# Graph attention on one core: which heads' probabilities VectorE turns, tile by tile, and exponentials that write a second buffer

## The chip, the core and the metric

The kernel runs on one core of a Trainium2 chip. Its time is the device time of one execution in microseconds (us), the median of several runs. The engines named below are TensorE (PE in the profile, with PEld for its weight loads), VectorE (DVE), ScalarE (ACT), GpSimd (POOL) and SyncE (SP), which here only issues DMAs.

## The reference

There are 16 graphs of 1024 nodes with 256 features, and two layers. Layer 0 is attention with 8 heads of 32, masked by the adjacency matrix; layer 1 weighs edges by a product of normed nodes. Both end in a softmax over 1024 columns and a weighted sum.

```
h = relu(layernorm(x))
Q, K, V = proj(Wq, bq), proj(Wk, bk), proj(Wv, bv)          # 8 heads of 32
scores = where(adj == 0, -inf, Q K^T * 32**-0.5)
x = x + (softmax(scores) V) Wo^T + bo
h = relu(layernorm(x))
e_k = leaky_relu((h * a_k) h^T);  scores = e_(adj-1), or -9e15 where adj == 0
x = x + softmax(scores) h
```

The change is in layer 0, between softmax and the product with V.

## The kernel before

**Tiles and steps.** Each graph is cut into 8 tiles of 128 rows (t = 0 to 7). The main loop runs over all 128 tiles, and inside it over 8 steps, one for each head h. The order of the work is written out by hand in this loop: every engine gets its instructions in the order in which the loop records them, and waits are put in where a buffer or a value needs it. Several tiles are in work at once: `now` makes scores, `was` is the tile before it, whose output is finished in steps 0 to 5, `edge` and `edge_was` are layer 1 of tiles nine and ten places back, and `piece` prepares layer 0's keys and values nine places ahead.

**One head.** In step h, TensorE makes the scores of head h (line 455), and VectorE adds the mask, takes the maximum and writes p (`softmax_max`, line 467). In step h + 1, ScalarE makes the exponential of p in place and its sum (`softmax_exp`, line 475). In step h + 2, p is turned, since the product with V needs the columns on the partitions. There are two ways to turn it:

- by TensorE: 8 transposes of 128 x 128 (line 574) into PSUM, which ScalarE copies out in two halves (line 575);
- by VectorE: one transposition of 32 x 32 blocks (`turn_blocks`, line 376) into one of three `blocks` buffers, after which SyncE issues four DMAs of 128 KB (`place_blocks`, line 381) that bring the blocks to their places in pT.

The second way leaves the columns in another order than the first. V is therefore stored in two orders: heads 0, 1, 4 and 5 in the one that suits VectorE's way, heads 2, 3, 6 and 7 in the plain one. `BY_BLOCKS = (0, 1, 4, 5)` says which heads go by VectorE, in every tile.

**Two gathers.** `combine(g)` (line 510) multiplies the turned heads of group g with V: 128 small matmuls for heads 0 to 3 in step 7 of the tile, for heads 4 to 7 in step 3 of the next one. In step 3 the order on ScalarE is the exponential of head 2, `recT` (line 504, the turned reciprocals of `was`), the bend of layer 1 (line 648), a copy to `mirror` (line 630), the flag of the next adjacency tile (line 447), and in step 4 the exponential of head 3. combine(1) writes the PSUM bank that `recT` is copied from. After it, VectorE makes oT (line 520) and TensorE the product with Wo (line 525); VectorE adds the rest (line 531) and takes statistics for the norm.

**Keys.** Each graph has 8 key tiles of 512 KB, one buffer for each head. They are loaded by SyncE (line 355) at the seam between two graphs: for heads 0 to 3 in tile 7 of the graph before, in steps 3, 4, 5 and 6, for heads 4 to 7 in tile 0, in steps 0, 2, 3 and 4. The queries of the next tile are loaded in step 3 (line 422). All these loads stand in one queue with the placing DMAs, the stores of the results (line 691) and of layer 0's output (line 536).

**Buffers.** p has 4 buffers, used in turn; pT has 7.

Of the kernel before, what the change touches and what calls it, by code (L numbers as in the profile page):

```python
# [8 lines left out]
F32 = mybir.dt.float32  # L9
# [4 lines left out]
AF = mybir.ActivationFunctionType  # L14
# [3 lines left out]
P = 128  # L18
HEADS = 8
HD = 32  # L20
# [3 lines left out]
SLOPE = 0.2  # L24
NEG_INF = -9000000000000000.0
MASKED = -1e30
BY_BLOCKS = (0, 1, 4, 5)


def place_of(h):  # L30
# [12 lines left out]
def gnn_kernel(  # L43
# [18 lines left out]
    nc = tc.nc  # L62
    B, N, D = x.shape
# [4 lines left out]
    NB = P // HD  # L68
# [10 lines left out]
    work = ctx.enter_context(tc.tile_pool(name="work", bufs=2))  # L79
# [330 lines left out]
    class Attend:  # L410
# [61 lines left out]

        def softmax_exp(self, h):
            p, nmx = self.probs[h]
            nc.scalar.activation(p, p, AF.Exp, bias=nmx, scale=-1.0, accum_out=self.sums[:, h : h + 1])  # L475

        def turn(self, h, half):
            if half == 0:
# [291 lines left out]
    with tc.manual_schedule():  # L770
# [48 lines left out]
        for s in range(B * NT + 1):  # L819
            b, t = divmod(s, NT)  # L820
# [8 lines left out]
            for h in range(HEADS):  # L829
                ending, eh = (now, h - 1) if h >= 1 else (was, HEADS - 1)  # L830
                turning, th = (now, h - 2) if h >= 2 else (was, HEADS + h - 2)
# [36 lines left out]
                if h == 3:  # L868
# [3 lines left out]
                        piece_was.biased()  # L872
                    if was:
                        was.combined()
                if turning and th in BY_BLOCKS:
                    turning.turn_blocks(th)
                    turning.place_blocks(th)
                elif turning:
                    turning.turn(th, 0)
                    turning.turn(th, 1)  # L880
# [75 lines left out]
            gone, was, now, nxt = was, now, nxt, nxt2  # L956
# [86 lines left out]
```

## Time and profile before

| | us |
|---|---|
| median of 3 runs | 3142.49 |
| lowest, highest | 3139.09, 3142.89 |
| the profiled execution | 3143.69 |
| its span | 3141.9 |
| busy in it: TensorE | 2941.3 (94%) |
| ScalarE | 2598.8 (83%) |
| VectorE | 2512.8 (80%) |
| GpSimd | 2172.4 (69%) |

The length of a tile, from the starts of line 467 for head 0, is on average over graphs 1 to 14: 29.1 us for tile 0, then 23.6, 23.1, 22.8, 22.6, 22.6, 22.4, and 22.3 for tile 7. In graph 0, where layer 1 has no work yet, tiles last 19.9 to 21.7 us.

Some durations of one instruction, mean: maximum of a head 1207 ns, exponential 1155 ns, VectorE's turn 1238 ns, TensorE's transpose 273 ns (eight of them overlap to 1.04 us), a copy of half a head 590 ns.

How to read the profile: busy shares are averages over tiles that have different limits, so the tiles at the seam and those in the middle have to be looked at by themselves. A row of the time line has the start in us, the duration in us, the engine and line, the operation, what it writes and reads, how many instructions are merged in it, and in brackets how long the engine was idle before it and what ended that. "SPq" is SyncE's queue; its duration is that of the issue, not of the transfer.

### The profile page before, as it was taken

How to read it: one execution, taken by the hardware profiler on the slowest of the kernel's cores; microseconds unless marked ns; L12 is line 12 of the kernel's file. 1: busy time of each engine (PE TensorE's matmuls, PEld its weight loads, DVE VectorE, ACT ScalarE, POOL GpSimd, SP SyncE). 2: the span in 40 equal slices, each digit the busy share in tenths (PEclk: the TensorE clock that was granted, in tenths of full speed). 3: DMA queues.
4: the chain of work that ended last, by engine and by line, in shares of the span. 5: the costliest groups of instructions: out<-in, count | busy, mean ns of one | idle time of the engine just before them, and what ended most of it. 6: DMA issues, size and time to landing. Idle time of an engine off the chain costs nothing. (4 is left out here: it accounts for less than half of the span.)

```text
span 3141.9 us, 95789 instructions
## 1 busy us (share of the span) xinstructions
PE 2941.3 (94%) x36210; PEld 2202.9 (70%) x36210; DVE 2512.8 (80%) x4391; ACT 2598.8 (83%) x5157; POOL 2172.4 (69%) x2995
## 2 busy tenths in 40 slices
PE   5888999899999999999999999999999999998987
PEld 3666777677676777777777676777767777676663
DVE  4777888788787887878888787888878788787874
ACT  3888989889888988889889898888978888787871
POOL 2666777777777776777777777777767777675542
PEclk8999999999999999999999999999999999999999
DMA  6676787877878787787877878787787877777663
GB/s 214 208 245 212 230 272 220 270 217 230 255 229 263 223 263 225 226 268 223 270 227 235 251 234 257 228 258 229 234 261 215 271 223 227 245 232 239 185 174 96
DMA packets 634692, 729.22 MB, mean 232 GB/s; under 512 B 67376, under 2 KB 565424, under 8 KB 634224
## 3 DMA queue, kind: packets, MB, share of 16 engines
q1 hardware_dynamic: 565152, 510.86, 54.5%
q0 software_dynamic: 66960, 210.04, 20.5%
q8 instruction: 291, 4.77, 0.6%
q10 hardware_dynamic: 2112, 2.10, 0.2%
q14 instruction: 177, 1.45, 0.1%
HBM read 252.98 MB, written 134.22 MB: 123 GB/s over the span
## 5 line engine op out<-in xcount | busy, mean ns | idle before, releaser
L467 DVE CUSTOM_DVE_ANT_0 p<-s,neg 128x1024 f32<-128x1024 f32 x1024 | 1235.6, 1207 | 274.5 <-PE s L455 241.3
L475 ACT ACTIVATE p<-p,nmx 128x1024 f32<-128x1024 f32 x1024 | 1182.2, 1155 | 205.0 <-DVE nmx L467 202.5
L455 PE MATMUL s<-k,qt 128*128 128x512 f32 x2048 | 764.9, 455 | 107.9 <-DMA k<-kd 72.5
L376 DVE STREAM_TRANSPOSE blocks<-p 128x1024 f32<-128x1024 f32 x520 | 643.7, 1238 | 20.5 <-ACT p L663 10.6
L575 ACT COPY pT<-trp 128x512 f32<-128x512 f32 x1024 | 547.0, 590 | 106.2 <-PE trp L574 106.2
L510 PE MATMUL acc<-pT,v 128*32 128x128 f32 x16384 | 559.0, 281 | 37.1 <-DMA pT<-blocks 22.1
L510 PEld LDWEIGHTS acc<-pT,v 128*32 128x32 f32 x16384 | 472.6, 113 | 156.5 <-issue 82.9
L574 PE MATMUL trp<-ident,p 128*128 128x128 f32 x4096 | 531.2, 273 | 1.6 <-ACT pT L575 1.5
L574 PEld LDWEIGHTS trp<-ident,p 128*128 128x128 f32 x4096 | 478.1, 140 | 73.2 <-ACT pT L575 3.1
L435 POOL TENSOR_SCALAR neg<-adj 128x1024 bf16<-128x1024 int32 x128 | 467.6, 3653 | 79.5 <-ACT neg L447 70.2
L681 PE MATMUL acc<-h,pT 128*32 128x256 f32 x8192 | 494.7, 383 | 8.8 <-DVE ot L690 8.8
L455 PEld LDWEIGHTS s<-k,qt 128*128 128x128 f32 x2048 | 324.3, 192 | 215.5 <-issue 79.5
L681 PEld LDWEIGHTS acc<-h,pT 128*32 128x32 f32 x8192 | 241.8, 110 | 211.9 <-issue 63.8
L659 POOL TENSOR_TENSOR sel<-sel,less 128x1024 f32<-128x1024 f32 x120 | 286.6, 2388 | 64.9 <-ACT less L648 44.9
L616 PE MATMUL s<-h1T,ha 128*128 128x512 f32 (+2 forms) x744 | 272.8, 490 | 2.6 <-ACT h1T L553 1.3
L657 POOL TENSOR_SCALAR less<-top 128x1 f32<-128x1 f32 x120 | 31.6, 264 | 274.5 <-DVE top L639 274.5
L319 POOL DMA_DIRECT2D qd<-halves x240 | 177.0, 777 | 58.7 <-POOL halves L309 31.8
L494 POOL COPY wide<-rec 128x256 f32<-128x256 f32 x128 | 53.9, 421 | 226.5 <-DVE rec L492 226.5
L475 ACT ACTIVATION_READ_ACCUMULATOR p<-p,nmx 128x1 f32 x1024 | 202.7, 198 | 0.0
L325 POOL DMA_DIRECT2D kd<-halves x240 | 171.7, 764 | 35.4 <-POOL halves L309 35.4
L309 POOL TENSOR_TENSOR halves<-full,halves 128x256 fp32r<-128x256 f32 x240 | 176.3, 735 | 20.6
L648 ACT ACTIVATE less<-sel 128x1024 f32<-128x1024 f32 x120 | 127.0, 1058 | 65.6 <-DVE top L639 65.6
(120 smaller groups left out, 4238.8 us busy)
## 6 DMA issues: line engine op xcount, KB each, us to landing
pT<-blocks SPq DMA_DIRECT2D x2560, 128.0 KB, 3.6
k<-kd SPq DMA_DIRECT2D x128, 512.0 KB, 6.1
qt<-qd SPq DMA_DIRECT2D x128, 512.0 KB, 4.4
adj<-in_adj POOLq DMA_DIRECT2D x127, 512.0 KB, 5.1
qd<-halves POOLq DMA_DIRECT2D x240, 256.0 KB, 3.0
kd<-halves POOLq DMA_DIRECT2D x240, 128.0 KB, 4.0
xb<-in_x POOLq DMA_DIRECT2D x128, 128.0 KB, 4.4
x1d<-x SPq DMA_DIRECT2D x128, 128.0 KB, 4.0
```

What stands on the lines that cost most here:

```text
L319: nc.gpsimd.dma_start(out=qds[self.b][self.first, oc].rearrange("p u w n -> p u (w n)"), in_=halves.unsqueeze(1).to_broadcast([P, 2, 2 * P]),)
L376: nc.vector.transpose(blocks.rearrange("p b j q -> p j b q"), p)
L435: nc.gpsimd.tensor_scalar(self.neg, self.adj, 0.0, MASKED, ALU.is_equal, ALU.mult)
L455: nc.tensor.matmul(self.ps[:, cols], lhsT=self.qt[:, h, :], rhs=keysets[self.b][h][:, cols], start=True, stop=True,)
L467: nc.vector.tensor_tensor_reduce(out=p, in0=sides[h in (4, 6)], in1=self.neg, scale=-SCALE, scalar=FLOOR, op0=ALU.add, op1=ALU.min, accum_ ...
L475: nc.scalar.activation(p, p, AF.Exp, bias=nmx, scale=-1.0, accum_out=self.sums[:, h : h + 1])
L510: nc.tensor.matmul(sums_place[r * HD : (r + 1) * HD, g * P : (g + 1) * P], lhsT=vs[self.b][:, j, place_of(h) : place_of(h) + HD], rhs=self ...
L574: nc.tensor.transpose(tr[:, j, :], p[:, jj * P : (jj + 1) * P], ident)
L575: copy(pT[:, half * 4 : half * 4 + 4, :], tr)
L616: nc.tensor.matmul(self.side[:, cols], lhsT=self.ha[:, c, :], rhs=h1T[:, c, cols], start=(c == 0), stop=(c == NC - 1),)
L659: nc.gpsimd.tensor_tensor(self.sel, self.sel, self.less, ALU.subtract)
L681: nc.tensor.matmul(sums_place[a * HD : (a + 1) * HD, :], lhsT=self.pT[:, j, a], rhs=h1s[self.b][:, j, :], start=(j == 0), stop=(j == NT - 1),)
```

## The change

The heads that VectorE turns now depend on the tile: heads 0 and 1 in tile 7, heads 4 and 5 in tile 0, heads 0, 1, 2, 4 and 5 in tiles 1 to 6. V's two orders stay as they are (`MIXED`). A head that is turned in the way that V's order is not made for has its columns put into the right order by the exponential: it reads p and writes a second buffer of the same four in the other order, instead of working in place. That concerns head 2 in tiles 1 to 6, heads 4 and 5 in tile 7, heads 0 and 1 in tile 0: ten exponentials of each graph's 64.

```diff
-BY_BLOCKS = (0, 1, 4, 5)
+MIXED = (0, 1, 4, 5)
+BY_BLOCKS = {7: (0, 1), 0: (4, 5), 1: (0, 1, 2, 4, 5), 2: (0, 1, 2, 4, 5), 3: (0, 1, 2, 4, 5), 4: (0, 1, 2, 4, 5), 5: (0, 1, 2, 4, 5), 6: (0, 1, 2, 4, 5)}
+
+
+def by_blocks(t):
+    return BY_BLOCKS.get(t, MIXED)
...
         def softmax_exp(self, h):
             p, nmx = self.probs[h]
-            nc.scalar.activation(p, p, AF.Exp, bias=nmx, scale=-1.0, accum_out=self.sums[:, h : h + 1])
+            to, of = p, p
+            if (h in MIXED) != (h in by_blocks(self.t)):
+                was = p
+                p = work.tile([P, N], F32, tag="p", bufs=4)
+                orders = "p (j q b) -> p j b q", "p (j b q) -> p j b q"
+                if h not in MIXED:
+                    orders = "p (j b q) -> p j q b", "p (j q b) -> p j q b"
+                to, of = (a.rearrange(order, b=NB, q=HD) for a, order in zip((p, was), orders))
+                self.probs[h] = p, nmx
+            nc.scalar.activation(to, of, AF.Exp, bias=nmx, scale=-1.0, accum_out=self.sums[:, h : h + 1])
...
-                if turning and th in BY_BLOCKS:
+                if turning and th in by_blocks(turning.t):
                     turning.turn_blocks(th)
                     turning.place_blocks(th)
                 elif turning:
```

In these orders b counts 4 and q counts 32: head 2 writes with 32 elements between neighbours, the four others with 4.

## The prediction

> **What bounds the kernel now.** I read four views in this order: the busy time by stretches of one graph's end, the time line of one tile, the SyncE queue, and the waits. Tile t (0 to 7) and head h (0 to 7) are the loops' numbers; "combine(1)" and "combine(0)" are the two gathers of line 510.
>
> The first view has one row for each of four neighbouring tiles (6, 7, then 0 and 1 of the next graph): stretch, its length, busy time of TensorE, weight loads, VectorE, ScalarE, GpSimd, then granted clock, DMA share, GB/s.
>
> ```profile
> 1122.20:1144.30 22.10, 21.99 (x285) 16.81 (x284) 19.37 (x34) 19.94 (x40) 15.65 (x20) 1.00 0.72 219
> 1144.30:1166.90 22.60, 21.93 (x286) 16.99 (x285) 19.54 (x34) 19.92 (x41) 18.86 (x29) 1.00 0.92 286
> 1167.00:1197.40 30.40, 24.81 (x286) 19.31 (x285) 19.56 (x34) 20.08 (x39) 20.65 (x30) 0.89 0.93 320
> 1197.40:1221.40 24.00, 23.86 (x286) 17.27 (x285) 19.70 (x35) 21.00 (x43) 15.08 (x21) 1.00 0.59 169
> ```
>
> Two regimes stand there. In tiles 1 to 7 TensorE is busy nearly throughout (21.99 of 22.10 us). In tile 0 it stands still for 5.6 us, at a clock of 0.89 and a DMA share of 0.93, although its work is the same. What it waits for there:
>
> ```profile
> PE s L455 <- DMA k<-kd: 72.5, 36, 5.8
> PE acc L510 <- DMA pT<-blocks: 22.1, 25, 2.2
> ```
>
> The next graph's keys come late because their loads stand in SyncE's queue behind the placing of heads turned by VectorE (four DMAs of about 0.62 us issue each):
>
> ```profile
> 1164.59 2.85 SPq L381 DMA_DIRECT2D pT<-blocks  x4
> 1167.48 0.63 SPq L536 DMA_DIRECT2D x1d<-x  x1
> 1168.16 0.52 SPq L355 DMA_DIRECT2D k<-kd  x1
> 1168.79 3.67 SPq L381 DMA_DIRECT2D pT<-blocks  x4
> 1172.56 0.93 SPq L355 DMA_DIRECT2D k<-kd  x1
> ```
>
> These fours are heads 4 and 5 of tile 7. The key behind the first lands at 1175.6, and scores(3) waits 2.35 us for it.
>
> In a middle tile the bound is not TensorE alone. Step 3 of a tile 6:
>
> ```profile
> 1127.93 1.24 DVE L376 STREAM_TRANSPOSE blocks<-p 128x1024 f32<-128x1024 f32 x1
> ...
> 1128.11 1.15 ACT L475 ACTIVATE p<-p,nmx 128x1024 f32<-128x1024 f32 x1 [0.41 <-DVE nmx L467]
> ...
> 1129.29 0.37 ACT L504 COPY recT<-acc 128x256 f32<-128x256 f32 x1
> 1129.71 1.78 PEld L510 LDWEIGHTS acc<-pT,v 128*32 128x32 f32 x61 [0.43 <-ACT recT L504]
> ```
>
> The first row is head 0's turn. The exponential of head 2 starts while it runs; recT follows on ScalarE, and combine(1) starts 0.05 us after recT. So this exponential is two instructions ahead of TensorE's next work.
>
> **The change, part by part.** I sum against the profiled execution (3143.7 us, span 3141.9), which is 1.2 us above the median shown, 3142.5.
>
> *Middle tiles (1 to 6 of 16 graphs: 96).* Head 2 goes from TensorE to VectorE.
>
> The added wait. In the changed program the exponential of head 2 writes a new p, and with four p in turn this is the place of head 0 of the same tile: the built program makes it wait for head 0's turn, the first row above. That ends 1.06 us after the exponential starts today; with 0.1 us for the signal (the gap from a maximum's end to its exponential) it starts 1.16 us later. Queued behind it on ScalarE are recT, the bend, the mirror copy, the flag and exp(3); combine(1) waits for recT, the scores of head 4 for the mirror copy. Today recT itself starts some time after exp(2) ends, because it waits for line 500: from the start times of lines 475 and 504, 0.76 us in tile 1, 0.35 in tiles 2 to 5, 0.03 in tile 6, where 0.03 is no slack. So combine(1) moves by 0.43, 0.84 and 1.16 us: mean (0.43 + 4 x 0.84 + 1.16) / 6 = **+0.83 us**.
>
> What is saved behind it, counted from combine(1)'s start. Eight transposes (1.04 us, 0.87 from their start to the next one's) leave TensorE, and two copies of 0.59 leave ScalarE. But the output product of line 525, next on TensorE, needs oT: oT starts at +2.30 and takes 0.42, so with 0.14 for the signal the product starts at +2.86 instead of +3.53. TensorE gains 0.67 and would reach combine(0) at +11.28 instead of +11.95 (median of the middle tiles). The rest of the 0.87 is a wait for oT that the transposes covered.
>
> What is late next: head 2 must now land by DMA before combine(0).
>
> ```profile
> 1133.73 2.49 SPq L381 DMA_DIRECT2D pT<-blocks  x4
> 1136.32 0.54 SPq L422 DMA_DIRECT2D qt<-qd  x1
> ```
>
> Head 1's four and the next queries fill SyncE from +4.02 to +7.15 (combine(1) is at 1129.71). VectorE turns head 2 after the maximum of head 4, from about +5.0 to +6.2, so it is ready before SyncE; its four DMAs issue from +7.2 to +9.7, the last at +9.1. Landing after issue:
>
> ```profile
> DMA to landing us min/median/max: 2.4/3.6/8.8
> ```
>
> That gives +11.5 to +12.7; heads 4 and 5, in a fuller queue, land 3.4 us after their last issue ends, which would be +13.1. I take +12.25: the queries just ahead land 4.2 us after their issue, at +10.8, DMAs land in their order, and the four follow at some 0.35 us each. So combine(0) comes at +12.25 instead of +11.95, **+0.30 us** (ends: -0.67, TensorE alone, and +1.15). VectorE's added 1.24 us (19.4 busy of 22.1) goes first into the 0.78 us it is idle before line 531 and delays the maximum of head 5 to +7.75 from +7.33; the scores of head 7, which need its place, stand at +10.6, so this costs nothing.
>
> Sum: 0.83 + 0.30 = 1.13 us, times 96 = **+108 us** (ends: 0.16 and 1.98 us, +15 and +190).
>
> The new orders of writing. 160 exponentials write in steps: head 2 with 128 bytes between elements, heads 0, 1, 4, 5 with 16. The nearest row is the mirror copy, which writes in 16-byte steps, beside a plain copy (mean ns after the busy time):
>
> ```profile
> L575 ACT COPY pT<-trp 128x512 f32<-128x512 f32 x1024 | 547.0, 590 | 106.2 <-PE trp L574 106.2
> L630 ACT COPY mirror<-s 128x512 f32<-128x512 f32 x64 | 36.4, 569 | 2.6 <-PE s L616 2.6
> ```
>
> No penalty at 16 bytes, so I take nothing. No row writes in 128-byte steps: the upper end is an estimate, the exponential's 1155 ns twice, +1.16 us each; the lower end is -0.09, the difference to the Relu of line 648, which does not write in place (1058). [...]
>
> *Tiles 7 and 0.* Heads 4, 5 of tile 7 and 0, 1 of tile 0 go to TensorE: eight transposes each, 1.04 us, with two copies on ScalarE (1.07 together). TensorE is the bound there, so each costs 1.04 (ends 0.87 and 1.2, where the copies set the pace): 64 heads x 1.04 = +67. Their exponentials find their place free long before. Sixteen placing DMAs leave the queue between these keys: the key issued at 1168.2 can go at about 1164.6, right behind the stores, and the next one after it instead of at 1172.6, before the scores need them; 2.1 MB less compete. Tile 0 lasts 29.4 us on average in graphs 1 to 15 (starts of line 467), 7.1 above tile 7's 22.3; I let 6.5 of it go (ends 5 and 7.1; part of it is the 0.89 clock): 15 x 6.5 = -98. Together **-31 us** (ends -51 and +2).
>
> Sum: 3143.7 + 108 - 31 = 3220.7, so **3220 us**, 2.5% slower.
>
> **Rivals.** (1) The boundary pays, which ends on the other side: head 2 lands in the shortest time seen, so TensorE alone counts in the middle tiles: 96 x 0.16 = +15, and the boundary gives about -38: 3121 us. It decides from 0.40 us per middle tile (38/96), that is a last landing before +11.5. For it: 2.4 us has been seen. Against it: that is the minimum, with queries just ahead. (2) Head 2 lands as late as heads 4 and 5: combine(0) at +13.1: 96 x 0.85 = 82 more, 3302 us. For it: the queries ahead; against it: head 1 lands 2.2 us after its last issue. (3) Stepped writing is dear: 96 x 1.16 = 111 more, 3332 us. Against it: the mirror row. (4) Both sides cancel: about 3145 us, with 0.4 us per middle tile. That the change does not do what it says is excluded: the built program has 32 more turns on VectorE and the waits named above.
>
> **How the numbers follow.** Forecast 0.62, rival 1 0.12, rival 2 0.12, rival 3 0.08, rival 4 0.06. A measurement of this kernel tells 0.2% (6 us) from no change. Slower: 0.62 + 0.12 + 0.08 = 0.82; same 0.06; faster 0.12. The range 3140 to 3310 holds the forecast with most of its own ends and rivals 2 and 4; outside are rivals 1 and 3, 2 in 10.
>
> **What would show it.** Right: in tiles 1 to 6 the third exponential starts after VectorE's turn, idle some 1.5 us before it; combine(1) waits longer for recT; combine(0) waits for pT from blocks; these tiles last near 23.7 us; tile 0 falls to about 25, tile 7 rises to about 24.4; the wait for keys nearly vanishes. Wrong: middle tiles of 22.6 us or less; the stepped exponentials far from 1.15 us; tile 0 still near 29.

## The result, and the profile after

| | us |
|---|---|
| before, median of 4 runs | 3142.69 (3139.09 to 3148.50) |
| after, median of 4 runs | 3616.28 (3608.71 to 3641.63) |
| ratio | 1.1525, 95% interval 1.1472 to 1.1578 |
| the profiled execution after | 3618.44, span 3616.6 |

The change makes the kernel 15% slower. The sign was forecast, the size was not: 3220 us, with 3140 to 3310 as the range.

In the changed program the lines of the code stand lower: the maximum is line 472, the exponential 489, VectorE's turn 381, the placing 386, the queries' load 427, the combines 524, recT 518, oT 534, the mirror copy 644.

Where the time went can be added up from the starts of line 472 for head 0. Over all 16 graphs, tiles 1 to 6 are longer by 495.6 us, tile 7 by 20.3, tile 0 is shorter by 42.5, and the stretch before the first tile is longer by 1.3; together 474.7, the difference of the two profiled spans (tile 7 includes what follows the last one). On average over graphs 1 to 14 the tiles last (us):

| tile | 0 | 1 | 2 | 3 | 4 | 5 | 6 | 7 |
|---|---|---|---|---|---|---|---|---|
| before | 29.1 | 23.6 | 23.1 | 22.8 | 22.6 | 22.6 | 22.4 | 22.3 |
| after | 26.6 | 28.9 | 28.2 | 26.5 | 26.2 | 27.2 | 27.9 | 23.8 |

A middle tile lasts 27.48 us instead of 22.85, so **4.63 us more** where the prediction had 1.13. The busy time by stretches answers to the first view of the prediction; these are tiles 5, 6 and 7 of one graph and 0 and 1 of the next (length, TensorE, weight loads, VectorE, ScalarE, GpSimd, clock, DMA share, GB/s):

```profile
1286.00:1314.10 28.10, 23.17 (x276) 16.78 (x274) 20.31 (x35) 20.12 (x38) 18.89 (x26) 0.95 0.78 237
1314.10:1339.10 25.00, 22.09 (x278) 16.65 (x277) 20.33 (x36) 20.08 (x38) 14.05 (x19) 0.98 0.62 176
1339.10:1363.30 24.20, 23.66 (x303) 18.78 (x302) 17.41 (x33) 22.73 (x43) 18.45 (x27) 1.00 0.92 290
1363.30:1389.70 26.40, 23.42 (x303) 17.97 (x301) 17.31 (x32) 24.02 (x45) 18.06 (x26) 1.00 0.64 217
1389.70:1418.10 28.40, 24.99 (x276) 17.69 (x275) 20.52 (x35) 20.86 (x41) 19.19 (x27) 0.94 0.75 221
```

The two regimes have changed places. Tile 0 (fourth row) stands still for 3.0 us at a clock of 1.00, where it was 5.6 at 0.89. The middle tiles, which were full, stand still instead: in the first row TensorE works 23.17 us of 28.10, in the last 24.99 of 28.40. The waits say for what (total, times, longest):

```profile
PE acc L524 <- DMA pT<-blocks: 301.7, 113, 7.2
...
PEld acc L524 <- ACT recT L518: 247.5, 128, 3.2
...
ACT p L489 <- DVE blocks L381: 135.8, 96, 2.0
```

The wait for keys, 72.5 us before, is no longer in that list. In its place the gathers wait 301.7 us for placing, head 2's above all (22.1 before, for the placing of others), and recT costs them four times as much as before (62.2). The last row is the new wait of the prediction, in all 96 middle tiles.

The time line of the first of these tiles, step 3 on ScalarE, VectorE and TensorE:

```profile
1291.69 1.24 DVE L381 STREAM_TRANSPOSE blocks<-p 128x1024 f32<-128x1024 f32 x1
...
1292.97 2.10 ACT L489 ACTIVATE p<-p,nmx 128x1024 f32<-128x1024 f32 x1 [1.51 <-DVE blocks L381]
...
1294.93 0.36 ACT L518 COPY recT<-acc 128x256 f32<-128x256 f32 x1
...
1295.34 2.16 PE L524 MATMUL acc<-pT,v 128*32 128x128 f32 x64 [1.54 <-ACT recT L518]
```

ScalarE waits for head 0's turn, as forecast; but then the exponential takes 2.10 us, not 1.15. Next, SyncE's queue in the same tile, with the queries' load and the placing of head 2 behind it:

```profile
1301.89 0.54 SPq L427 DMA_DIRECT2D qt<-qd  x1
1302.60 2.56 SPq L386 DMA_DIRECT2D pT<-blocks  x4
```

The first gather of a middle tile before the change, and then TensorE's rows for it in this tile:

```profile
1141.67 1.95 PE L510 MATMUL acc<-pT,v 128*32 128x128 f32 x64
```

```profile
1306.64 0.41 PE L524 MATMUL acc<-pT,v 128*32 128x128 f32 x4
1310.32 2.50 PE L524 MATMUL acc<-pT,v 128*32 128x128 f32 x60 [3.27 <-DMA pT<-blocks]
```

combine(0) is ready at 1306.64, 11.30 us after combine(1) began (the forecast said 11.28; the median of the middle tiles is 11.30). It does four of its 64 matmuls and then stands for 3.27 us: the four DMAs, issued from 1302.60 to 1305.16, land between 1307.80 and 1310.19. What the DMA engines and the clock did meanwhile, in the same columns as above:

```profile
1297.50:1301.50 4.00, 4.00 (x37) 2.87 (x40) 3.86 (x6) 3.54 (x9) 3.92 (x3) 1.00 0.29 75
1301.50:1304.00 2.50, 2.50 (x40) 1.29 (x36) 2.40 (x6) 1.72 (x6) 2.35 (x3) 1.00 0.70 194
1304.00:1307.00 3.00, 3.00 (x38) 1.74 (x29) 2.80 (x7) 2.84 (x5) 2.70 (x6) 1.00 0.97 310
1307.00:1310.30 3.30, 0.05 (x2) 0.01 (x1) 2.46 (x4) 2.42 (x6) 2.96 (x8) 1.00 1.01 277
1310.30:1313.00 2.70, 2.68 (x61) 2.32 (x62) 0.00 (x0) 0.00 (x0) 2.19 (x4) 0.73 1.00 363
```

From 1304 on the DMA share is 0.97 to 1.01. After the standstill the granted clock averages 0.73 over 2.7 us; it falls to 0.50 at 1311.55 and is back at 1.00 at 1314.97. On average over the middle tiles of graphs 1 to 14 the longest gap in combine(0), from one matmul's start to the next, is 2.83 us, and from first to last matmul it lasts 5.61 us instead of 1.95. The tile shown is one of the worse: head 2's last DMA lands 14.85 us after combine(1) began, 14.12 on average.

The clock is a part of the loss by itself. In 52 of the 96 middle tiles it falls to 0.50, in none before, and it stays there for 293 us of them in all. Between the first tile and the last it falls 58 times, 35 times for 3.41 us, 19 for 6.83, once for 10.24 and three times for 13.65. By the profile's busy times, TensorE was busy for 0.49 or less of the 3.41 us ahead of each fall; of the 861 other stretches of that length, after which the clock stayed at 1.00, TensorE was busy for at least half in 838. In the tile shown TensorE was busy for 1.23 of the 3.41 us ahead of the fall at 1311.55, so a standstill of 3.27 us, shorter than such a stretch, was enough there.

### The profile page after: what moved, and what is told of

Same layout as the page of the kernel before. It is cut to its first block, busy times and chain, and to the rows that moved or that the text cites. A ratio compares the mean times of both kernels' runs of the same rounds, so it can differ in the third digit from the quotient of the medians.

```text
span 3616.6 us, 95204 instructions
## 1 busy us (share of the span) xinstructions
PE 3041.2 (84%) x35954; PEld 2252.7 (62%) x35954; DVE 2534.2 (70%) x4423; ACT 2696.7 (75%) x5093; POOL 2169.4 (60%) x2995
## 5 line engine op out<-in xcount | busy, mean ns | idle before, releaser
L489 ACT ACTIVATE p<-p,nmx 128x1024 f32<-128x1024 f32 x1024 | 1347.3, 1316 | 272.9 <-DVE nmx L472 136.0
L524 PE MATMUL acc<-pT,v 128*32 128x128 f32 x16384 | 647.5, 301 | 465.0 <-DMA pT<-blocks 301.7
L524 PEld LDWEIGHTS acc<-pT,v 128*32 128x32 f32 x16384 | 541.4, 121 | 595.8 <-issue 297.1
L589 ACT COPY pT<-trp 128x512 f32<-128x512 f32 x960 | 518.7, 599 | 452.6 <-PE trp L588 452.4
L460 PE MATMUL s<-k,qt 128*128 128x512 f32 x2048 | 776.7, 461 | 29.5 <-DMA qt<-qd 15.2
L381 DVE STREAM_TRANSPOSE blocks<-p 128x1024 f32<-128x1024 f32 x552 | 683.4, 1238 | 10.7 <-ACT p L677 10.6
L588 PE MATMUL trp<-ident,p 128*128 128x128 f32 x3840 | 514.8, 278 | 25.1 <-ACT pT L589 25.1
L588 PEld LDWEIGHTS trp<-ident,p 128*128 128x128 f32 x3840 | 454.8, 144 | 114.7 <-ACT pT L589 44.7
L534 DVE TENSOR_TENSOR oT<-acc,recT 128x256 f32<-128x256 f32 x128 | 54.2, 423 | 224.4 <-ACT mirror L644 108.6
L489 ACT ACTIVATION_READ_ACCUMULATOR p<-p,nmx 128x1 f32 x1024 | 210.8, 206 | 0.0
```

The costliest lines, as they stand in the source:

```text
L381: nc.vector.transpose(blocks.rearrange("p b j q -> p j b q"), p)
L460: nc.tensor.matmul(self.ps[:, cols], lhsT=self.qt[:, h, :], rhs=keysets[self.b][h][:, cols], start=True, stop=True,)
L489: nc.scalar.activation(to, of, AF.Exp, bias=nmx, scale=-1.0, accum_out=self.sums[:, h : h + 1])
L524: nc.tensor.matmul(sums_place[r * HD : (r + 1) * HD, g * P : (g + 1) * P], lhsT=vs[self.b][:, j, place_of(h) : place_of(h) + HD], rhs=self ...
L588: nc.tensor.transpose(tr[:, j, :], p[:, jj * P : (jj + 1) * P], ident)
L589: copy(pT[:, half * 4 : half * 4 + 4, :], tr)
```

## The experiments

**The theory** after the traces: three causes in the middle tiles, each with its own price. Steps: the exponential that writes a second buffer in another order takes 2.1 us instead of 1.15. Wait: it also waits for head 0's turn. Landing: head 2's blocks come late, at a DMA share of 0.97 to 1.01. **The rivals**: the landing alone sets the tile, whatever comes before it; or the added transfers slow everything; and, for the seam, its stepped exponentials eat its gain. Tile lengths below are means over tiles 1 to 6 of graphs 1 to 14, and an experiment without an interval is one execution. The four executions of the changed kernel lie 33 us apart, 0.34 us per middle tile if all of it lies there, so differences of that size between single executions order nothing.

### The price of a step, by itself

Single operations on 128 x 1024 numbers, six in a row, source and target in SBUF or PSUM.

```
step4  = "p (j q b) -> p j b q"   # neighbours 16 bytes apart
step32 = "p (j b q) -> p j q b"   # neighbours 128 bytes apart
step2  = the same with b = 2      # neighbours 8 bytes apart
```

> This kernel leaves out the whole computation: it times single operations on 128 x 1024 fp32, six of each in a row. What costs the extra microsecond of a stepped exponential? Theory 1 (writing in steps to SBUF is dear when the source is SBUF too): the exponential contiguous 1.15 us in place and 1.06 to 1.15 out of place; writing in 16-byte steps 2.25, in 128-byte steps 2.11; from PSUM all three near 1.1 to 1.2, as the mirror copy showed (569 ns against 590); reading in steps free. [...] Theory 3 (the sum of the two reorderings, reading and writing): reading in steps also costs about 1 us. VectorE's transposition, 1.24 us plain: 1.24 with 16-byte reads by theory 1, about 2.3 by theory 3.

The groups by line (busy time, mean ns). L59 is the exponential in order, L63, L65 and L67 write in steps of 16, 128 and 8 bytes, L69 and L71 read SBUF in steps of 16 and 128, L75 and L77 write the two steps from PSUM; L85 is VectorE's turn, L87 the same with a source in steps:

```profile
L69 ACT ACTIVATE res<-src,bias 128x1024 f32<-128x1024 f32 x6 | 12.6, 2105 | 0.2
L63 ACT ACTIVATE res<-src,bias 128x1024 f32<-128x1024 f32 x6 | 12.5, 2089 | 0.2
L75 ACT ACTIVATE res<-ps,bias 128x1024 f32<-128x1024 f32 x6 | 12.3, 2052 | 0.2
L65 ACT ACTIVATE res<-src,bias 128x1024 f32<-128x1024 f32 x6 | 12.3, 2049 | 0.2
L71 ACT ACTIVATE res<-src,bias 128x1024 f32<-128x1024 f32 x6 | 12.3, 2048 | 0.2
L77 ACT ACTIVATE res<-ps,bias 128x1024 f32<-128x1024 f32 x6 | 12.0, 1992 | 0.2
...
L87 DVE STREAM_TRANSPOSE blocks<-res 128x1024 f32<-128x1024 f32 x6 | 11.9, 1983 | 0.2
...
L85 DVE STREAM_TRANSPOSE blocks<-res 128x1024 f32<-128x1024 f32 x6 | 7.5, 1246 | 137.8 <-ACT res L83 137.6
...
L67 ACT ACTIVATE res<-src,bias 128x1024 f32<-128x1024 f32 x6 | 7.2, 1207 | 0.2
L59 ACT ACTIVATE res<-src,bias 128x1024 f32<-128x1024 f32 x6 | 6.9, 1147 | 0.2
```

Theory 1, that the source matters, falls: steps into SBUF cost the same from PSUM (2052) as from SBUF (2089). What theory 3 says of ScalarE holds: an SBUF side, read or written, with neighbours 16 or 128 bytes apart costs 0.88 to 0.96 us per 1024 elements. VectorE's turn pays 0.74 for reading in 16-byte steps, less than theory 3 said (1.98 us instead of 2.3). Steps of 8 bytes cost 0.06. A copy from PSUM that writes 16-byte steps takes 1951 ns as well. That left the row on which the prediction had rested, the mirror copy at 569 ns, without an explanation. A second kernel looked for it, with the steps in PSUM, on either side, and with runs of 16 and 8 bytes written to SBUF:

> This kernel leaves out the whole computation: it times single operations on 128 x 1024 fp32, six of each in a row. [...] Theory 2 (any step costs on ScalarE, and the mirror copy was fast for another reason, its 512 elements or its operation): PSUM in steps takes 2.0 to 2.1 as well.

L72, L74 and L76 read PSUM in order and in steps of 128 and 16 bytes; L78, L80 and L82 write PSUM in the same three ways, each in 1118 ns; L84 and L86 write SBUF in runs of 16 and of 8 bytes; L90 is VectorE's copy in steps of 128 bytes:

```profile
L86 ACT ACTIVATE res<-src,bias 128x1024 f32<-128x1024 f32 x6 | 7.1, 1178 | 0.2
L84 ACT ACTIVATE res<-src,bias 128x1024 f32<-128x1024 f32 x6 | 6.9, 1150 | 0.2
L78 ACT ACTIVATE ps<-src,bias 128x1024 f32<-128x1024 f32 x6 | 6.7, 1118 | 0.2
...
L72 ACT ACTIVATE res<-ps,bias 128x1024 f32<-128x1024 f32 x6 | 6.7, 1115 | 3.5 <-DVE ps L70 3.3
L74 ACT ACTIVATE res<-ps,bias 128x1024 f32<-128x1024 f32 x6 | 6.7, 1115 | 0.2
...
L90 DVE COPY res<-src 128x1024 f32<-128x1024 f32 x6 | 6.6, 1097 | 0.2
```

Theory 2 of this run falls: PSUM in steps costs ScalarE nothing, read (1115 and 1114 ns against 1115) or written (1118 in each order). It is SBUF in steps that took 1992 to 2105 in the kernel above; runs of 16 and 8 bytes into SBUF take 1150 and 1178. VectorE's copy takes 1097 ns instead of 694. And the mirror copy is now read rightly. Its code is

```
nc.scalar.copy(
    place.rearrange("p j (k b) -> p j k b", b=NB),              # written: k, then b: in order
    blocks.rearrange("p (j b k) -> p j k b", b=NB, k=HD),       # read from PSUM: b is 128 bytes apart
)
```

so its steps lie in PSUM, on the reading side; it writes SBUF in order. It said nothing of stepped writing.

### The seam alone

```diff
-BY_BLOCKS = {7: (0, 1), 0: (4, 5), 1: (0, 1, 2, 4, 5), ... 6: (0, 1, 2, 4, 5)}
+BY_BLOCKS = {7: (0, 1), 0: (4, 5)}
```

> Only tiles 7 and 0 are changed; tiles 1 to 6 turn heads 0, 1, 4, 5 by VectorE as before. If the loss lies in the middle tiles alone (theory A), the seam gives what the traces differ by there: tile 0 shorter by 2.7 us (15 times, -41), tile 7 longer by 1.46 (16 times, +23), so about 3125 us (3110 to 3135). If the stepped exponentials of the seam eat its gain (theory D), 3145 to 3170.

3125.01 us (3122.69 to 3129.29), ratio 0.9949 (0.9932 to 0.9965). Middle tiles 22.81, tile 0 26.44, tile 7 24.11. So theory A: the loss lies wholly in the middle tiles, and the seam part by itself gains 17 us.

### Without the landing

```diff
-                        rhs=self.turned[h][:, j],
+                        rhs=self.turned[1 if h == 2 and 0 < self.t < 7 else h][:, j],
```

> As the changed kernel, head 2 still turned and placed by VectorE and SyncE in tiles 1 to 6, but the first gather multiplies head 1's turned probabilities in head 2's place there, so that it no longer waits for head 2's landing; head 2's product is left out. Theory A (three causes: stepped exponential, wait for the second p, late landing): the gap of 2.2 to 3.3 us in the gather and the slower clock after it go, 3.0 to 3.7 us in each of 96 tiles, 3260 to 3330 us; about 1 us per tile stays. Theory B (the landing is the whole loss): 3175 to 3200. Theory C (the extra transfers slow everything): near 3600.

Head 1's turned probabilities stand in for head 2's, so head 2's product is left out; the number of matmuls is the same. 3265.7 us, middle tiles 24.03: 3.45 us less than after. combine(0) is back at 1.96 us from first to last matmul, and the granted clock of the whole run rises from 0.953 to 0.981. That is theory A, within its range; B said 3175 to 3200 us, C near 3600.

### Without steps and second p

V's columns hold heads 0, 1, 4, 5, 2, 3, 6, 7, so the half in VectorE's order can be widened by head 2.

```diff
-MIXED = (0, 1, 4, 5)
+MIXED = (0, 1, 2, 4, 5)
...
-                for i, hT in enumerate((self.hTm, self.hT)):
+                for cols, hT in ((slice(0, 5 * HD), self.hTm), (slice(5 * HD, D), self.hT)):
...
```

> As the changed kernel, but V holds head 2 in VectorE's order, so that in tiles 1 to 6 all five heads are exponentiated in place: no stepped writing and no second p in the middle tiles; instead head 2 of tiles 7 and 0 (32 exponentials) writes steps. The placing of head 2 stays. Theory A: combine(1) comes 1.6 to 2.1 us earlier against the third maximum, the wait for the landing stays 2 to 3 us, so 1.6 to 2 us of 96 tiles less, 30 us more at the seam: 3450 to 3500 us. Theory B (the landing sets the tile whatever comes before it): the time goes into a longer wait for head 2, 3580 to 3620. If wait and steps were most of it: below 3300.

3473.5 us, middle tiles 25.27: 2.21 us less than after. The landing's gap is still 2.34 us. Again A. At the seam the edit costs something: there head 2 is turned by TensorE and now needs a stepped exponential, and tile 7 lasts 27.19 and tile 0 27.62 us, against 24.11 and 26.44 in the seam alone. So one stepped exponential with its second buffer, in front of recT, goes with some 3 us in tile 7.

### Without steps, with the second p

```diff
                 to, of = (a.rearrange(order, b=NB, q=HD) for a, order in zip((p, was), orders))
+                if h not in MIXED:
+                    to, of = p, was
```

> As the changed kernel, but the exponential of head 2 in tiles 1 to 6 writes the second p in the order in which it reads, so the wait for the second buffer stays and the steps go (head 2's product is then made with V's rows in another order). Theory A (each cause counts by itself): this exponential takes 1.15 us instead of 2.11, combine(1) starts 0.96 us earlier, 96 times: 3520 to 3535 us. Theory B (the landing of head 2 sets the tile, and comes when it comes): the time goes into a longer wait for head 2, 3600 to 3620. If the steps also slow what follows: 3400 to 3480.

3532.35 us, middle tiles 26.61: 0.87 us less than after, close to the 0.96 by which the exponential became shorter. (V's rows stand in another order than head 2's columns here, so its product is not the reference's.) The step from here to the run above (26.61 to 25.27), 1.34 us, is what the second p costs, its wait above all.

### Why the landing is late

Two edits of order alone, each in one queue.

```diff
                 if h == 3:
-                    if nxt:
-                        nxt.load_queries()
...
                 if h == 4:
+                    if nxt:
+                        nxt.load_queries()
```

> As the changed kernel, but SyncE loads the next tile's queries (512 KB) behind the four placing DMAs of head 2 instead of ahead of them. Theory A1 (head 2 lands late because the queries' transfer is ahead of it in the same queue): head 2 lands 1.5 to 2.5 us earlier, the gap in the first gather falls from 2.8 to about 1 us, 3380 to 3470 us. Theory A2 (the transfers of GpSimd's queue at the same time, 512 KB of queries written and 512 KB of adjacency read, are what slows it): only the 0.5 us of issue is gained, 3560 to 3600. Theory B (VectorE turns head 2 too late): no change, 3600 to 3640.

3503.58 us, between the ranges of A1 and A2; middle tiles 26.23. Head 2's last DMA now lands 2.78 us after its issue ends, instead of 3.79, and the placing begins 0.65 us after the turn's end instead of 1.34; the gap in combine(0) falls from 2.83 to 1.11 us. That is the mechanism of A1, but the tile gains only 1.25: the queries, moved back, come late in their turn. The gathers' wait for placing falls from 301.7 to 128.4 us, but the scores' wait for queries rises from 15.2 to 100.1:

```profile
PE s L460 <- DMA qt<-qd: 100.1, 78, 14.9
```

The second edit:

```diff
                 if h == 4:
...
-                    if piece_was:
-                        piece_was.write_queries()
...
-                    if nxt2:
-                        nxt2.load()
...
                 if h == 6:
+                    if piece_was:
+                        piece_was.write_queries()
+                    if nxt2:
+                        nxt2.load()
```

> As the changed kernel, but GpSimd issues its write of the queries of the next graph and the adjacency load of the tile after next in step 6 instead of step 4, so that they are not under way while head 2 is placed. Theory A1 (the queries' load ahead in SyncE's queue is what makes head 2 late): 3560 to 3620 us. Theory A2 (sharing with GpSimd's transfers): head 2 lands 1.5 to 2.5 us earlier, 3380 to 3470. It may cost something in step 6 and 7, where heads 4 and 5 are placed.

3458.55 us, middle tiles 25.69, in A2's range: the landing after the last issue falls from 3.79 to 2.65 us, with the placing issued as late as before (1.33), and the gap to 1.67. So both are causes of the late landing: the queries ahead in the same queue, and GpSimd's transfers beside it. But moved transfers delay something else: head 4's placing, which shares step 6 with them now, lands 5.67 us after its last issue instead of 4.83.

### All of it together

First the last three edits in one kernel: V's wider half, the queries' load behind head 2, GpSimd's transfers in step 6.

> V in VectorE's order for head 2 too (no stepped exponentials in tiles 1 to 6), the queries' load behind the placing of head 2, and GpSimd's transfers in step 6. Theory A (steps, wait for p and landing are the three causes, and nothing else): the middle tiles fall to 22.5 to 23.5 us, tile 7 stays near 27 and tile 0 near 27.5 because of the stepped head 2 there: 3170 to 3260 us. If there is a further cause, such as VectorE's added 1.24 us of work in each middle tile: above 3300.

3327.28 us, which the expectation put down to a further cause. Middle tiles 24.08 instead of 22.5 to 23.5. The landing of head 2 is down to 2.16 us and the gap in combine(0) to 0.53, but combine(1) now has a gap of 0.88 (0.13 in the changed kernel), and head 4's placing lands 5.95 us after its last issue. The transfers were not taken away, only moved to the other gather.

Then V's wider half together with head 1 in head 2's place in the first gather:

> V in VectorE's order for head 2 (so no steps and no second p in tiles 1 to 6), and the first gather of these tiles uses head 1's turned probabilities in head 2's place, which leaves head 2's product out. So all three suspected causes are gone from the middle tiles, and VectorE's added turn, the four DMAs and TensorE's saved transposes stay. If the three add up as they did one by one (2.21 and 3.45 us from 27.48): middle tiles of 21.8 us, about 1 us below the kernel before, 3140 us in all (tile 7 and tile 0 keep a stepped head 2 that costs them 3.4 and 1.1). If VectorE's added turn or the scores' order is the next bound: 22.5 to 23 us and 3210 to 3255.

3182.31 us, between the two expectations; the middle tiles, 22.75, are those of the second. As above, head 2's product is left out. The sizes don't add up: one by one, steps and wait were worth 2.21 and the landing 3.45, together 5.66; with all taken away the tile is shorter by 4.73. What the first two delay is thus in part the same time that the landing costs. The clock's loss explains little of the difference of 0.93: in the middle tiles the clock stands at 0.50 for 293 us in the changed kernel, 75 without the landing, 194 without steps and second p, 14 without all three, and if half of that time is lost, these four make up 0.2 of the 0.93 us per tile (an estimate, and an upper one). And with all three causes gone a middle tile is as long as before the change (0.10 us shorter over graphs 1 to 14, 0.02 over all 16, which is no difference that single executions show): the eight transposes that TensorE is spared, and the turn that VectorE does in their place, gain nothing here.

### The seam's parts, and a version that is faster

```diff
-            if (h in MIXED) != (h in by_blocks(self.t)):
+            if False:
```

(on top of the seam alone; these heads' products are made with V's rows in another order and are not the reference's)

> Only tiles 7 and 0 are changed, and the heads out of V's order are exponentiated in place and in order (their product is then made with V's rows in another order): what do the 64 stepped exponentials and second buffers of the seam cost? If ScalarE has room there: 3115 to 3125 us, as the seam with them (3125). If each costs its extra 1.1 us on the path: 3050 to 3070.

3095.17 us (3093.64 to 3102.55), ratio 0.9863 (0.9828 to 0.9897), between the expectations. Tile 7 stays at 24.11, tile 0 falls from 26.44 to 24.36. So tile 7's stepped exponentials cost nothing, and those of heads 0 and 1 in tile 0 cost 2.08 us with their second buffers.

Then each tile by itself, `{7: (0, 1)}` and `{0: (4, 5)}`:

> VectorE turns heads 0 and 1 alone in tile 7; all other tiles as before. If the placing DMAs of tile 7's heads 4 and 5, which stand in SyncE's queue between the keys, are what makes tile 0 late: tile 7 longer by 1.8 us, tile 0 shorter by 3 to 5, about 3100 to 3125 us. If tile 0's own placing counts as much: tile 0 shorter by only 1 to 2, 3140 to 3155.

> VectorE turns heads 4 and 5 alone in tile 0; all other tiles as before. If the delay comes from tile 7's placing, tile 0 keeps its stall and its added transposes fall into it: 3140 to 3160 us. If tile 0's own eight placing DMAs delay keys 4 to 7: 3105 to 3130.

Tile 7 alone: 3099.98 us (3095.92 to 3109.50), ratio **0.9879** (0.9842 to 0.9917), tile 7 23.99 and tile 0 24.95. Tile 0 alone: 3118.34 (3111.66 to 3119.87), ratio 0.9924 (0.9898 to 0.9950), tile 0 27.29. The first time is at the edge of its first case (3100 to 3125), the second lies within its second (3105 to 3130): tile 7's placing delays the keys, and tile 0's own does too. Which does more isn't shown. Tile 0 alone shortens tile 0 by 1.83 us against 4.17, but it has the stepped exponentials of heads 0 and 1 in that tile; if they cost the 2.08 from above, the placing itself is worth 3.9 (an estimate). Tile 7 alone is the fastest version found that computes the reference, 1.2% below the kernel before, and faster than both parts together: it takes the placing out of the queue between the first keys, and its stepped exponentials are those that cost nothing. The wait for keys is half of before's 72.5 in it (16.2 in tile 0 alone):

```profile
PE s L460 <- DMA k<-kd: 36.0, 17, 6.5
```

Last, one head of tile 7 at a time, `{7: (0, 1, 5)}` and `{7: (0, 1, 4)}`:

> In tile 7 head 4 alone goes to TensorE (heads 0, 1, 5 by VectorE), all other tiles as before. If one placing out of the queue between the keys is enough: tile 7 longer by 0.8 us, tile 0 shorter by 3.5 to 4, about 3085 to 3100 us. If each of the two counts half: tile 0 shorter by 2, 3115 to 3125.

> In tile 7 head 5 alone goes to TensorE (heads 0, 1, 4 by VectorE), all other tiles as before. If one placing out of the queue between the keys is enough: 3085 to 3100 us. If each of the two counts half: 3115 to 3125. If head 4's placing, the earlier one, is the one that matters: 3130 or more here, and head 4 alone gives nearly all.

3106.48 us, ratio 0.9900 (0.9862 to 0.9938), and 3108.89, ratio 0.9900 (0.9866 to 0.9934); tile 0 25.57 and 25.86, tile 7 23.19 and 23.27. Both lie between the expectations, and the third case of head 5, that head 4's placing alone matters (3130 or more), falls: either head alone takes most off tile 0 (3.55 and 3.26 us, 4.17 with both), at half the price in tile 7. The intervals of these two and of both heads together overlap, so no order among the three is shown.

## Why the prediction was wrong, by its steps

- **The bounds of the kernel before**: right. The seam stood on the keys, and the middle tiles on ScalarE's order in step 3 as much as on TensorE.
- **The added wait, +0.83 us**: right. Behind head 0's turn the exponential starts late, after 1.4 us of idle time on average (135.8 us in 96 waits). From the end of one tile's combine(0) to the next combine(1) it is 8.86 us before, 9.76 with a second p written in order, and 10.55 in the changed kernel: +0.90 for the wait, +0.79 for the steps. To take the second p away is worth more, 1.34 us, since combine(0) then becomes shorter too (4.89 us instead of 5.53).
- **The saving on TensorE, -0.67**: combine(0) was ready at 11.30 us, as worked out (11.28). But in a tile where nothing else is late it gains nothing that shows (22.75 us against 22.85).
- **The landing, +12.25 us after combine(1), and so +0.30 us per tile**: this step failed most. From combine(1)'s start to combine(0)'s end it is 2.91 us more, 16.90 instead of 13.99: a gap of 2.83, and 0.8 more for the 64 matmuls, which then run in part at a clock of 0.50, less the 0.75 by which combine(0) begins earlier on average. These 2.91 and the 1.69 above are the loss of a middle tile. The prediction gave the lower clock to tile 0 alone. The issue was nearly right, +7.2 to +9.7 forecast, +7.26 to +9.82 in the tile shown, +7.5 to +10.3 on average. The landing was not: +14.85 in that tile and +14.12 on average, 3.79 us after the last issue's end where the forecast let 2.55 pass. The prediction took the 4.2 us of the queries' load from the trace of before and let the four follow at 0.35 us each; it did not read the DMA share at that moment. In the tile shown, the queries (512 KB), head 2 (512 KB) and GpSimd's write of queries (512 KB) are all issued between 1301.89 and 1306.1; at the 277 to 310 GB/s of the rows above, these 1.57 MB take some 5.1 to 5.7 us (an estimate). The queries landed 5.5 us after their issue, and the four DMAs took 5.2 to 6.3 us each (4.3 on average over the middle tiles, where the median of the trace before was 3.6). Alone, the landing costs 2.52 us (25.27 against 22.75), with the other two present 3.45.
- **The stepped exponentials, 0, with +1.16 as the upper end**: this step failed too, by a misread row. The mirror copy reads PSUM in steps and writes SBUF in order. The steps cost 0.96 us in the exponential (2.11 instead of 1.15), 0.87 per middle tile, and at the seam 2.08 in tile 0. By bytes between neighbours, steps of 8 cost 60 ns on 1147, steps of 16 cost 942 and steps of 128 cost 902.
- **The seam, -31 us**: -17 as built. Without the steps it is -45, within the stated ends: tile 7 +1.79 per graph where 2.08 was said, tile 0 -4.76 where -6.5 + 2.08 = -4.42 was said. So the seam's sum was good, and what it lacked is the steps, valued at nothing.
- **The rivals**: the second (head 2 lands late) and the third (steps are dear) were given 0.12 and 0.08 as if only one of them could happen. Both happened, and the first was over twice its size: combine(0) ends 2.91 us later against combine(1), where rival 2 had 1.15. Both added to the forecast, at the prices given, make some 3414 us; most of what is left to 3616 is the size of the landing.
- **The signs**: the late exponential, the wait of combine(0) and the end of the wait for keys came as said. Tile 0 fell to 26.6 us, not to 25. "Near 23.7" for the middle tiles was a slip: 22.85 + 1.13 is 24.0.
- **The graphs at the ends** were counted like the others. Graph 0's six middle tiles grew by 62.8 us together, over 10 us each, and graph 15's by 43.9, where graphs 1 to 14 grew by 27.8 on average. Why is not shown.

## What to carry to other kernels

Before a row is used as the price of an access pattern, read in the code which side of it is in steps and which memory that side lies in: here ScalarE took 1114 ns where it read PSUM in 16-byte steps, 2105 where it read SBUF in them. When a product is moved from an engine to DMA, the landing is not the issue time plus a usual latency (here a DMA of 128 KB took 2.5 to 2.7 us at a share of 0.29 to 0.70, and 5.2 to 6.3 where it rose to 0.97 to 1.01): add up the bytes that every queue has under way at that moment, and read the DMA share of that stretch. A standstill of TensorE costs more than its length where the clock falls after it (here 2.83 us, and 0.8 in the matmuls behind it). And a two-instruction path ahead of the bound engine (here exp(2), recT) is the wrong place for an instruction that both waits and becomes longer; the same edit in tile 7's heads 4 and 5 cost nothing.

## What the runs showed of the hardware

- ScalarE, 128 x 1024 fp32: SBUF read or written with neighbours 16 or 128 bytes apart takes 1.99 to 2.11 us instead of 1.15; PSUM read or written in the same steps takes 1.11 to 1.12, as in order.
- The exponential that writes to PSUM takes 1118 ns, the one that reads PSUM 1115, the one within SBUF 1147.
- VectorE's block transposition takes 1983 ns instead of 1246 when it reads in 16-byte steps, and its copy 1097 instead of 694 when it writes in 128-byte steps. GpSimd's copy takes 1954 instead of 1041 when it reads in 128-byte steps.
- A standstill of TensorE of 3.3 us was followed by a granted clock of 0.73 over 2.7 us; with head 2's landing taken out of the gather the mean clock of the run rose from 0.953 to 0.981. A DMA share of 0.92 alone did not lower it: tile 7 in the rows above ran at 1.00. In the changed kernel's trace each of the 58 falls of the clock came after 3.41 us in which TensorE was busy for 0.49 or less of the time.
- A placing DMA of 128 KB landed 2.5 to 2.7 us after its issue at a DMA share of 0.29 to 0.70 (head 1 in the tile shown), and 5.2 to 6.3 us after it where the share rose to 0.97 to 1.01 (head 2).
- In both traces SyncE's DMAs, 3098 and 3226, all landed in the order of their issue.
